# Stage 3 of a two-layer perceiver: keys and queries in a PSUM bank of their own, the end of the attention in two halves, three evictions on ScalarE, the recurrence's first exponentials ahead of the scaling by D

## The chip, the cores and the metric

One core of a Trainium2 chip runs the whole program. The metric is the device time of one execution in microseconds (us). The kernel before took 2087.88 us, the median of three runs that went from 2087.57 to 2094.29.

The core's engines each run their own list of instructions in order: TensorE (PE, with its weight loads shown as PEld), VectorE (DVE), ScalarE (ACT), GpSimd (POOL) and SyncE (SP), which here issues most DMA. Matmul results land in PSUM, which has eight banks of 512 fp32 columns on 128 partitions. "Evicting" a bank means reading it into SBUF.

## The reference

The input x is 64 sequences of 32 tokens with 256 features, 2048 tokens in all; a context of 64 x 257 rows belongs to it. Six residual steps follow one another:

```python
x = x + _L0_xattn_ref(_layernorm(x), ctx, ctx, mask, ...)   # stage 0
x = x + _L0_attn_ref(_layernorm(x), ...)                    # stage 1
x = x + _L0_ffn_ref(_layernorm(x), ...)                     # stage 2
x = x + _L1_xattn_ref(_layernorm(x), ctx, wq, wk, wv, wo, ln_gamma, ln_beta)   # stage 3
x = x + _L1_attn_ref(_layernorm(x), ...)                    # stage 4
x = x + _L1_ffn_ref(_layernorm(x), ...)                     # stage 5
```

The change concerns stages 3 and 4. Stage 3 is grouped-query attention, 16 query heads over 8 key heads of 16 features, with quantised linear maps (each row is scaled to integers up to 127, each weight matrix to -1, 0, 1):

```python
q = bit_linear(x, wq); k = bit_linear(y, wk); v = bit_linear(y, wv)
scores = einsum('bhgnd,bhsd->bhgns', q / 4, k)      # s runs over 257 context rows
out = einsum('bhgns,bhsd->bhgnd', softmax(scores), v)
out = layernorm(out) * ln_gamma + ln_beta
return bit_linear(out, wo)
```

Stage 4 is a selective state-space layer, with 512 channels and 16 states:

```python
h = exp(A * dt) * h + dt * B_t * x_t        # for every time step t
y_t = sum_n h[n] * C_t[n] + D * x_t
y = (y * silu(z)) @ out_proj.T + out_proj_b  # then residual and layernorm
```

## The kernel before

**Tiling.** The 2048 tokens are four blocks of 512 (`NBLK`), a block is four tiles of 128 tokens, and a tile is four sequences ("elements", e) of 32 tokens. `layers` (at the end of the listing) calls the stages block by block. Stages 0 and 1 come first; block 0 of stages 2 and 3 lies beside the last blocks of stage 1. Then stage 3 of block b+1 is called beside the recurrence of block b, and stage 5 of block b-1 after it. Stage 4 has three parts: `ahead` (normalise, project, convolve, step sizes dt), `gates` (silu of z) and `recur`.

**What sets the order.** The kernel is written for a planner that orders each engine's instructions at compile time: what is written earlier has priority, and an instruction whose operands and buffers are free by the planner's costs may come before earlier ones that wait. It puts in all the waits. Every buffer is a tile of a pool under a tag with a number of copies (`bufs`); a tile gets a copy when an earlier tile of the same tag is released.

**PSUM.** From stage 4 on, four pools hold the banks: psh (2, the recurrence's h), psp (1, projections of `ahead` and `gates`), psu (1, stage 5's), psacc (2, stage 5's sums), and, from stage 3 on, ps (2), from which every tile of stage 3 comes.

**Stage 3.** `block` normalises and quantises four tiles into xq and opens o4, the output, in the same buffer (tag xn3, one copy). It then takes nine half-tile steps u. In each, for two elements, `keys` projects keys (kT, L823, evicted on DVE at L825 with the quantisation steps) and values (v, L830, evicted on DVE at L836); `scores` is called for two pairs of heads (matmuls L844, maxima L849 and L851 on DVE, exponentials L855 on ACT); between these two calls, `sums` is called for the step before (transposes L868, copies L870 on ACT, value matmuls L878, evictions od L882 on ACT and L883 on DVE). A new tile begins with `attend`: loads of cq and kb, xqT (L776), q (L781, evicted on DVE at L783), the context's last row (L787 to L795), qT (L800, evicted twice on DVE at L804 into qm) and the last row's scores (L807). `back` ends a tile: softmax denominators, transposes, the write into o4 (L918 to L923). The end of the block, L738 to L764, works on four tiles at once: layernorm, gamma and beta on POOL (L743, L744), quantisation, output projection, residual add (L764).

**Stage 4.** In `recur`, dtx = dt * x is one POOL instruction (L1044), the first step of every sequence is set so that its exponential is zero (L1046), and four ACT instructions scale y by D (L1049). Then for each of 16 states and each pair of channel groups come g on POOL (L1056), exponentials h on ACT (L1060), the scan and the product hc on DVE (L1061, L1062) and the addition to y on POOL (L1063).

Small helpers: `_stats` and `_rsqrt` (L69 to L92) compute means and reciprocal roots with a dozen POOL instructions on four numbers a row; `_norm` (L115) applies them; `_quant_rows` (L340 to L350) scales and rounds.

## Time and profile before

| what | value |
|---|---|
| median of three runs | 2087.88 us |
| the profiled execution's own time | 2087.24 us |
| its span, first to last instruction | 2085.2 us |
| PE busy | 1597.6 us (77%) |
| DVE busy | 1384.2 us (66%) |
| POOL busy | 1049.5 us (50%) |
| ACT busy | 944.1 us (45%) |
| mean granted TensorE clock | 0.832 |

The profile is one execution, recorded by the hardware. A row of a group gives line, engine, operation, output and inputs, shape and count, then the total busy time, the mean duration of one in ns, and the idle time of its engine just before it with what ended that. A row of the timeline gives start and duration in us. A row of one line's instructions gives the shortest, median and longest duration in ns, and the first and last start in us. The busy time of PE includes waiting in its pipeline, so a busy PE need not be at its peak.

### The profile page before, as it was taken

The numbers are of one execution on the slowest core, as the hardware profiler recorded it, in microseconds if no ns is written. First come the engines' busy times: TensorE is split into PE (matmuls) and PEld (weight loads), VectorE is DVE, ScalarE is ACT, GpSimd is POOL, SyncE is SP. The second block draws the span as 40 slices with busy tenths as digits, with TensorE's granted clock in tenths as the row PEclk, the third lists the DMA queues.
The fourth block names the chain that finished last, engine by engine and source line by source line (L and its number), as shares of the span: only waits on it lengthen the run. The fifth ranks groups of instructions, "written<-read, shape, count | busy, mean of one in ns | idle before, by whom it ended". The sixth has DMA issues, their size and how long they took to land. (4 is left out here: it accounts for less than half of the span.)

```text
span 2085.2 us, 20012 instructions
## 1 busy us (share of the span) xinstructions
PE 1597.6 (77%) x6323; PEld 812.4 (39%) x6323; DVE 1384.2 (66%) x2443; ACT 944.1 (45%) x2001; POOL 1049.5 (50%) x1069
## 2 busy tenths in 40 slices
PE   4776967667979788657387789877888787787798
PEld 3333534334545434433144344433344433233343
DVE  4588585765485568888777888775787844877100
ACT  2454352303445264434136466447566536564232
POOL 5344646413121324668724677732677843999100
PEclk9676968778989989657697789988699997899799
DMA  6754333300001010122002232102222212342121
GB/s 221 228 189 141 102 109 104 100 4 21 21 21 42 20 47 21 51 59 63 10 15 83 66 106 86 46 21 87 71 81 71 52 31 77 87 115 72 39 81 41
DMA packets 88376, 151.23 MB, mean 73 GB/s; under 512 B 7740, under 2 KB 52300, under 8 KB 86224
## 3 DMA queue, kind: packets, MB, share of 16 engines
q1 hardware_dynamic: 85428, 148.75, 23.4%
q10 hardware_dynamic: 2844, 1.22, 0.2%
q8 instruction: 50, 0.82, 0.2%
q14 instruction: 54, 0.44, 0.1%
HBM read 139.03 MB, written 10.92 MB: 72 GB/s over the span
## 5 line engine op out<-in xcount | busy, mean ns | idle before, releaser
L1056 POOL TENSOR_TENSOR g<-dtx,bc 128x1024 f32<-128x1024 f32 x128 | 300.4, 2352 | 191.4 <-DVE h L1061 101.7
L1061 DVE TENSOR_TENSOR_SCAN h<-h,g 128x512 f32<-128x512 f32 x256 | 308.1, 1219 | 47.0 <-ACT h L1060 28.7
L1063 POOL TENSOR_TENSOR xc<-xc,hc 128x1024 f32<-128x1024 f32 x128 | 301.0, 2354 | 34.5 <-DVE hc L1062 29.5
L1167 PE MATMUL up<-xT,w 128*128 128x512 f32 x512 | 288.4, 678 | 33.1 <-ACT hid L1169 29.6
L1175 PE MATMUL acc<-hid,w 128*128 128x512 f32 x512 | 258.0, 624 | 19.9 <-ACT hid L1171 19.9
L1060 ACT ACTIVATE h<-dt,A 128x512 f32<-128x512 f32 x256 | 173.9, 692 | 173.5 <-DVE hc L1062 172.3
L1062 DVE TENSOR_TENSOR hc<-h,bc 128x512 f32<-128x512 f32 x256 | 170.1, 681 | 5.8 <-POOL xc L1063 3.0
L1169 ACT ACTIVATE hid<-up,chan 128x512 f32<-128x512 f32 x128 | 87.2, 681 | 179.2 <-PE up L1167 179.2
L855 ACT ACTIVATE p<-sc,nm 128x256 f32<-128x256 f32 x256 | 117.7, 471 | 95.3 <-DVE nm L851 90.5
L1167 PEld LDWEIGHTS up<-xT,w 128*128 128x128 f32 x512 | 97.7, 209 | 157.3 <-issue 84.6
L630 PE MATMUL weps<-we,xT 128*128 128x512 f32 x256 | 140.0, 671 | 23.3 <-DVE x L632 14.7
L868 PE MATMUL pt_ps<-ident,p 128*128 128x128 f32 x512 | 95.9, 325 | 73.6 <-ACT p L855 36.3
L1175 PEld LDWEIGHTS acc<-hid,w 128*128 128x128 f32 x512 | 96.5, 199 | 137.8 <-issue 99.3
L844 PE MATMUL sc<-kT,qm 32*128 32x256 f32 x512 | 133.9, 447 | 4.9 <-DVE kT L825 2.4
L849 DVE TENSOR_REDUCE nm<-sc 128x2 f32<-128x512 f32 x128 | 86.2, 686 | 56.1 <-PE sc L844 55.1
L868 PEld LDWEIGHTS pt_ps<-ident,p 128*128 128x128 f32 x512 | 67.3, 163 | 123.0 <-ACT p L855 79.1
L89 POOL TENSOR_TENSOR rs_t<-rs_r 128x4 f32<-128x4 f32 (+3 forms) x138 | 33.3, 243 | 160.4 <-DVE rs_r L87 142.5
L844 PEld LDWEIGHTS sc<-kT,qm 32*128 32x128 f32 x512 | 82.7, 207 | 62.6 <-issue 10.8
L1188 DVE SCALAR_TENSOR_TENSOR o<-rT,gt,x 128x256 f32<-128x256 f32 x16 | 7.7, 483 | 133.2 <-PE rT L1187 124.0
L870 ACT COPY pt<-pt_ps 128x512 f32<-128x512 f32 x128 | 74.2, 588 | 32.9 <-PE pt_ps L868 32.3
L1044 POOL TENSOR_TENSOR dtx<-xc,dt 128x2048 f32<-128x2048 f32 x4 | 18.0, 4502 | 138.9 <-DVE dt L1030 127.4
L247 POOL TENSOR_TENSOR cT<-cT,scb 128x2056 f32<-128x2056 f32 x16 | 73.2, 4572 | 25.8 <-PE scT_ps L237 11.5
(389 smaller groups left out, 3166.0 us busy)
## 6 DMA issues: line engine op xcount, KB each, us to landing
bc<-rows SPq DMA_DIRECT2D x64, 512.0 KB
w<-in_L_ffn_w_dram SPq DMA_DIRECT2D x64, 512.0 KB
cT<-in_ctxT_dram SPq DMA_DIRECT2D x16, 1028.0 KB
cq<-cq SPq DMA_DIRECT2D x32, 514.0 KB
cn<-in_ctx_dram SPq DMA_DIRECT2D x64, 256.0 KB
scb<-scales SPq DMA_DIRECT2D x16, 514.0 KB
kb<-steps SPq DMA_DIRECT2D x16, 514.0 KB
x<-in_x_dram SPq DMA_DIRECT2D x4, 512.0 KB
```

Source lines behind the costliest of these rows:

```text
L630: nc.tensor.matmul(ps, xT[:, c, r], we[:, c, e : e + 2, :], start=c == 0, stop=c == 1)
L844: nc.tensor.matmul(sc[h][:, f, :], qm[r, e + f].rearrange("p l n g -> p (l n g)"), kTs[e][r, f, :], start=True, stop=True,)
L855: nc.scalar.activation(w_[:, f, h - h0, :], sc[h][:, f, :], AF.Exp, bias=nm[:, e + f, h : h + 1], accum_out=sm[:, e + f, h : h + 1],)
L868: nc.tensor.transpose(pt_ps[:, h, m, :], ws[e0, hp][:, f, h, m * P : (m + 1) * P], k.ident)
L1056: nc.gpsimd.tensor_tensor(g, dtx[:, c2 : c2 + 2], bc[:, 0:1, :].to_broadcast([P, 2, BT]), ALU.mult)
L1060: nc.scalar.activation(h, dt, AF.Exp, scale=A[:, c2 + c, n : n + 1])
L1061: nc.vector.tensor_tensor_scan(h, h, g[:, c, :], 0.0, ALU.mult, ALU.add)
L1062: nc.vector.tensor_tensor(hc[:, c, :], h, bc[:, 1, :], ALU.mult)
L1063: nc.gpsimd.tensor_tensor(y[:, c2 : c2 + 2], y[:, c2 : c2 + 2], hc, ALU.add)
L1167: nc.tensor.matmul(u, w1[e][:, c, q * P : (q + 1) * P], xT[:, c, :], start=c == 0, stop=c == 1)
L1169: nc.scalar.activation(hid[e][:, q, :], u, AF.Identity, bias=b1)
L1175: nc.tensor.matmul(acc[o], w2[e][:, q, o * P : (o + 1) * P], hid[e][:, q, :], start=n == H, stop=n == E * H + H - 1)
```

## The change

- Stage 3 gets a function `pk`, which takes a tile from the pool psp (one bank). The tiles of queries, the last row, keys and values come from it. Where psp is not open yet (block 0), they still come from ps.
- Stage 4's `ahead` takes its tiles from ps instead of psp, and `gates` from psu.
- q, qm and v are evicted on ScalarE: q and qm with one instruction in the place of each one before, v with four instructions of 128 columns in the place of one.
- `sums` handles both elements of a step in one call: one PSUM tile oT for both, two od evictions in the place of four.
- The end of a block becomes a function `finish` over two tiles: it runs to the quantised rows and returns `out`, the output projection and residual add. Tiles 0 and 1 are finished at u = 4 and projected at u = 6; tiles 2 and 3 after the last step.
- dtx is computed in two halves, the first on DVE, the second on POOL. The scaling by D moves into the state loop's first turn, behind the first two channel groups' scans and ahead of their addition to y.
- Small statistics tiles take the number of tiles they are given instead of 4, some get a tag of their own or one copy (rank, rp, rsm, rt), and the quantised end rows yq get a buffer of their own instead of sharing that of xq.

```diff
--- before.py
+++ after.py
...
@@ -700,6 +700,10 @@
+    def pk(shape, name, dt=F32):
+        return k.psp.tile(shape, dt, name=name, tag="p") if k.psp else ps(shape, name, dt)
     def block(b):
...
@@ -728,40 +732,51 @@
                 last.sums(le)
-                last.sums(le + 1)
             if u < 8:
...
                 last.back()
-        ot = [o4[:, j].rearrange("p i l g d -> p (i l g d)") for j in range(4)]
+            if u == 4:
+                ends = [finish(xs, o4, 0)]
+            if u == 6:
+                ends[0]()
+        finish(xs, o4, 2)()
+    def finish(xs, o4, j0):
+        js = range(j0, j0 + 2)
+        ot = [o4[:, j].rearrange("p i l g d -> p (i l g d)") for j in js]
         mv, rstd = _stats(k, ot, "3b")
-        y = o4.rearrange("p j i l g d -> p j (i l g d)")
-        for j in range(4):
-            _norm(k, ot[j], ot[j], mv, rstd, j)
-        nc.gpsimd.tensor_tensor(y, y, gamma.unsqueeze(1).to_broadcast([P, 4, D]), ALU.mult)
-        nc.gpsimd.tensor_tensor(y, y, beta.unsqueeze(1).to_broadcast([P, 4, D]), ALU.add)
-        ss = k.small.tile([P, 4], F32, name="ss", tag="q_ss")
-        yq = k.wk3.tile([P, 4, D], BF16, name="yq", tag="xq", bufs=1)
-        for j in range(4):
-            nc.scalar.activation(yq[:, j, :], y[:, j, :], AF.Square, accum_out=ss[:, j : j + 1])
-        am = k.small.tile([P, 4], F32, name="am", tag="q_am")
+        y = o4[:, j0 : j0 + 2].rearrange("p j i l g d -> p j (i l g d)")
+        for f in range(2):
+            _norm(k, ot[f], ot[f], mv, rstd, f)
+        nc.gpsimd.tensor_tensor(y, y, gamma.unsqueeze(1).to_broadcast([P, 2, D]), ALU.mult)
+        nc.gpsimd.tensor_tensor(y, y, beta.unsqueeze(1).to_broadcast([P, 2, D]), ALU.add)
+        ss = k.small.tile([P, 2], F32, name="ss", tag="q_ss")
+        yq = k.wk3.tile([P, 2, D], BF16, name="yq", tag="yq", bufs=1)
+        for f in range(2):
+            nc.scalar.activation(yq[:, f, :], y[:, f, :], AF.Square, accum_out=ss[:, f : f + 1])
+        am = k.small.tile([P, 2], F32, name="am", tag="q_am2")
         _quant_rows(k, y, 1e-8, yq, am)
-        dy = k.small.tile([P, 4], F32, name="dy", tag="dy")
+        dy = k.small.tile([P, 2], F32, name="dy", tag="dy")
         _rsqrt(k, dy, [(ss, 1.0 / D, RMS_EPS)], "3y")
...
         nc.vector.tensor_scalar(dy, dy, 1e-5, osc, ALU.max, ALU.mult)
-        for j in range(4):
-            yqT_ps = ps([P, 2, P], "yqT_ps", BF16)
-            for c in range(2):
-                nc.tensor.transpose(yqT_ps[:, c, :], yq[:, j, c * P : (c + 1) * P], k.identb)
-            yqT = k.wk3.tile([P, 2, P], BF16, name="yqT", tag="xqT")
-            nc.scalar.copy(yqT, yqT_ps)
-            wo_ps = ps([P, D], "wo_ps")
-            for c in range(2):
-                nc.tensor.matmul(wo_ps, yqT[:, c, :], wo[:, c, :], start=c == 0, stop=c == 1)
-            nc.vector.scalar_tensor_tensor(xs[j], wo_ps, dy[:, j : j + 1], xs[j], ALU.mult, ALU.add)
+        def out():
+            for f in range(2):
+                yqT_ps = ps([P, 2, P], "yqT_ps", BF16)
+                for c in range(2):
+                    nc.tensor.transpose(yqT_ps[:, c, :], yq[:, f, c * P : (c + 1) * P], k.identb)
+                yqT = k.wk3.tile([P, 2, P], BF16, name="yqT", tag="xqT")
+                nc.scalar.copy(yqT, yqT_ps)
+                wo_ps = ps([P, D], "wo_ps")
+                for c in range(2):
+                    nc.tensor.matmul(wo_ps, yqT[:, c, :], wo[:, c, :], start=c == 0, stop=c == 1)
+                x = xs[j0 + f]
+                nc.vector.scalar_tensor_tensor(x, wo_ps, dy[:, f : f + 1], x, ALU.mult, ALU.add)
+        return out
...
@@ -771,18 +786,18 @@
-        xqT_ps = ps([P, 2, P], "xqT_ps", BF16)
+        xqT_ps = pk([P, 2, P], "xqT_ps", BF16)
         for c in range(2):
...
         nc.scalar.copy(xqT, xqT_ps)
-        q_ps = ps([P, D], "q_ps")
+        q_ps = pk([P, D], "q_ps")
         for c in range(2):
...
         q = k.wk3.tile([P, D], F32, name="q", tag="q_ol", bufs=1)
-        nc.vector.tensor_scalar(q, q_ps, dq[:, j : j + 1], None, ALU.mult)
-        last_ps = ps([P, P + 4], "last_ps")
+        nc.scalar.activation(q, q_ps, AF.Copy, scale=dq[:, j : j + 1])
+        last_ps = pk([P, P + 4], "last_ps")
         for c in range(2):
...
@@ -795,14 +810,14 @@
         )
-        qT_ps = ps([P, 2, 4, T], "qT_ps")
+        qT_ps = pk([P, 2, 4, T], "qT_ps")
         for h in range(2):
...
         for l in range(2):
-            nc.vector.tensor_scalar(qm[:, :, l].rearrange("p e n g -> p g e n"), qT_ps, half[:, l : l + 1], None, ALU.mult)
-        sl_ps = ps([P, 4, 4], "sl_ps")
+            nc.scalar.activation(qm[:, :, l].rearrange("p e n g -> p g e n"), qT_ps, AF.Copy, scale=half[:, l : l + 1])
+        sl_ps = pk([P, 4, 4], "sl_ps")
         for e in range(4):
...
@@ -818,12 +833,12 @@
-            kT_ps = ps([P, 2, 2 * P], "kT_ps")
+            kT_ps = pk([P, 2, 2 * P], "kT_ps")
             for c in range(2):
...
             nc.vector.tensor_tensor(kTs[e], kT_ps, kb[:, e : e + 2, 0 : 2 * P], ALU.mult)
-            v_ps = ps([P, 2, 2, P], "v_ps")
+            v_ps = pk([P, 2, 2, P], "v_ps")
             for m in range(2):
...
@@ -833,7 +848,9 @@
             cd = k.cdq[:, :, g].rearrange("p (m e) -> p m e", m=2)[:, :, e : e + 2]
-            nc.vector.tensor_tensor(vs[e], v_ps, cd.unsqueeze(3).to_broadcast([P, 2, 2, P]), ALU.mult)
+            for m in range(2):
+                for f in range(2):
+                    nc.scalar.activation(vs[e][:, m, f, :], v_ps[:, m, f, :], AF.Copy, scale=cd[:, m, f : f + 1])
...
@@ -858,33 +875,34 @@
         def sums(e):
-            e0, f = e - e % 2, e % 2
-            pts = []
-            for hp in range(2):
-                pt_ps = ps([P, 2, 2, P], "pt_ps")
-                for h in range(2):
-                    for m in range(2):
-                        nc.tensor.transpose(pt_ps[:, h, m, :], ws[e0, hp][:, f, h, m * P : (m + 1) * P], k.ident)
-                pt = k.wk3.tile([P, 2, 2, P], F32, name="pt", tag="pt")
-                nc.scalar.copy(pt, pt_ps)
-                pts.append(pt)
-            oT_ps = ps([P, 2, 2 * T], "oT_ps")
-            ob = oT_ps.rearrange("p l q -> p (l q)")
-            for m in range(2):
-                for h in range(4):
-                    r = slice(32 * h, 32 * h + 32)
-                    nc.tensor.matmul(
-                        ob[r], vs[e0][:, m, f, r], pts[h // 2][:, h % 2, m, :],
-                        start=m == 0, stop=m == 1, skip_group_check=True,
-                    )
-            nc.scalar.activation(od4[:, e], oT_ps[:, 0], AF.Copy, scale=half[:, 0:1])
-            nc.vector.scalar_tensor_tensor(od4[:, e], oT_ps[:, 1], half[:, 1:2], od4[:, e], ALU.mult, ALU.add)
+            oT_ps = ps([P, 2, 2, 2 * T], "oT_ps")
+            for f in range(2):
+                pts = []
+                for hp in range(2):
+                    pt_ps = ps([P, 2, 2, P], "pt_ps")
+                    for h in range(2):
+                        for m in range(2):
+                            nc.tensor.transpose(pt_ps[:, h, m, :], ws[e, hp][:, f, h, m * P : (m + 1) * P], k.ident)
+                    pt = k.wk3.tile([P, 2, 2, P], F32, name="pt", tag="pt")
+                    nc.scalar.copy(pt, pt_ps)
+                    pts.append(pt)
+                ob = oT_ps[:, f].rearrange("p l q -> p (l q)")
+                for m in range(2):
+                    for h in range(4):
+                        r = slice(32 * h, 32 * h + 32)
+                        nc.tensor.matmul(
+                            ob[r], vs[e][:, m, f, r], pts[h // 2][:, h % 2, m, :],
+                            start=m == 0, stop=m == 1, skip_group_check=True,
+                        )
+            o2 = od4[:, e : e + 2]
+            nc.scalar.activation(o2, oT_ps[:, :, 0], AF.Copy, scale=half[:, 0:1])
+            nc.vector.scalar_tensor_tensor(o2, oT_ps[:, :, 1], half[:, 1:2], o2, ALU.mult, ALU.add)
...
-            rp = k.small.tile([P, 2, 4, 4], F32, name="rp", tag="rp3")
+            rp = k.small.tile([P, 2, 4, 4], F32, name="rp", tag="rp3", bufs=1)
             rs, pl = rp[:, 0], rp[:, 1]
...
@@ -965,7 +983,10 @@
     def pp(shape, name):
-        return k.psp.tile(shape, F32, name=name, tag="p")
+        return k.ps.tile(shape, F32, name=name, tag="s")
+    def pz(shape, name):
+        return k.psu.tile(shape, F32, name=name, tag="u")
...
@@ -1035,18 +1056,17 @@
         for c in range(C):
-            nc.scalar.activation(v.zs[:, c, :], project(v, C + c, pp), AF.Silu, bias=_chan(k, "L1_attn_in_proj_b", C + c))
+            nc.scalar.activation(v.zs[:, c, :], project(v, C + c, pz), AF.Silu, bias=_chan(k, "L1_attn_in_proj_b", C + c))
...
         dtx = wk.tile([P, C, BT], F32, name="dtx", tag="dtx", bufs=1)
-        nc.gpsimd.tensor_tensor(dtx, y, dt.unsqueeze(1).to_broadcast([P, C, BT]), ALU.mult)
+        for c2, eng in ((0, nc.vector), (2, nc.gpsimd)):
+            yc = y[:, c2 : c2 + 2]
+            eng.tensor_tensor(dtx[:, c2 : c2 + 2], yc, dt.unsqueeze(1).to_broadcast([P, 2, BT]), ALU.mult)
         nc.gpsimd.memset(dt.rearrange("p (b t) -> p b t", t=T)[:, :, 0:1], 1e20)
-        for c in range(C):
-            nc.scalar.activation(y[:, c, :], y[:, c, :], AF.Copy, scale=_chan(k, "L1_attn_D", c))
         bc_rows = v.rows[0 : 2 * N].rearrange("(two n) t -> n two t", two=2)
...
@@ -1060,6 +1080,10 @@
                     nc.vector.tensor_tensor(hc[:, c, :], h, bc[:, 1, :], ALU.mult)
+                if n == 0:
+                    for c in range(c2, c2 + 2):
+                        nc.scalar.activation(y[:, c, :], y[:, c, :], AF.Copy, scale=_chan(k, "L1_attn_D", c))
                 nc.gpsimd.tensor_tensor(y[:, c2 : c2 + 2], y[:, c2 : c2 + 2], hc, ALU.add)
...
@@ -1205,6 +1229,7 @@
     left0, left, right, right2 = ExitStack(), ExitStack(), ExitStack(), ExitStack()
+    k.psp = None
     with left0:
...
```

## The prediction

> **What bounds it now.** I read the page's strip of busy tenths first: no engine is full for long, so the time lies in chains, and these are found by asking where a stage starts and ends. Layer 1's attention (stage 3) handles a block of four token tiles. Its score matmuls (L844), asked for in three stretches of time, give the first and last start of blocks 1, 2 and 3:
>
> ```profile
> L844 PE MATMUL sc<-kT,qm x128: 374/478/792, 747.7 to 976.0; 32*128 32x256 f32 x128
> L844 PE MATMUL sc<-kT,qm x128: 374/374/791, 1076.1 to 1318.2; 32*128 32x256 f32 x128
> L844 PE MATMUL sc<-kT,qm x128: 374/374/791, 1388.7 to 1635.4; 32*128 32x256 f32 x128
> ```
>
> The blocks stand end to end, 313 to 328 us apart, because the next one needs the buffer xn3 that the last one's output o4 holds. Block 1's last residual add (L764) starts at 1043.8, block 2's mean is subtracted (L711) from 1038.5; block 3's from 1368.5. After block 3's last L764 (1690.5) come stage 4 of block 3 (first scan 1750.7, last 1906.8) and stage 5 to the end. So from 704 on the end is set by the attention's own latency, three blocks long, then by a tail of 394 us.
>
> The windows tell how much room an engine has in that chain (columns: window, length, busy us and instructions of PE, weight loads, DVE, ACT, POOL, then granted clock and DMA):
>
> ```profile
> 714.00:1119.00 405.00, 276.30 (x1199) 144.83 (x1198) 318.14 (x605) 169.82 (x379) 214.20 (x214) 0.76 0.16 44
> 1119.00:1691.00 572.00, 464.93 (x1956) 230.70 (x1955) 434.01 (x708) 323.83 (x654) 366.49 (x295) 0.85 0.22 65
> 1691.00:2085.00 394.00, 322.81 (x729) 137.72 (x727) 171.09 (x251) 180.18 (x215) 183.41 (x158) 0.90 0.24 70
> ```
>
> DVE is at 79% in the first, PE at 81% in the second: latency bounds, with one engine not far behind. Within the attention, the timeline of block 3 at the start of its fourth tile shows one line of work through the two banks of the pool ps:
>
> ```profile
> 1575.74 0.28 PE L776 MATMUL xqT_ps<-identb,xq 128*128 128x128 bf16 x2
> ...
> 1582.83 0.59 PE L823 MATMUL kT_ps<-cq,b_L_xattn_wkvT 128*128 128x512 bf16 x2
> ...
> 1585.81 1.67 PE L844 MATMUL sc<-kT,qm 32*128 32x256 f32 x8
> ```
>
> Query preparation takes 7.1 us, keys and values 3.0, and no score runs meanwhile. Each half-tile step (two elements' scores, exponentials, sums) takes some 33 us: 1389 to 1655 over eight.
>
> **The change, part by part (us for one of blocks 1, 2, 3; minus is gain).**
>
> Own bank. Queries, keys and values go to the bank psp. Tile n+1's queries still wait for qm (one buffer), which is free after tile n's last score matmul, so they run under its reductions and exponentials. The three preparations after the first took 6 to 7.1 us in block 3: -20. Keys to scores on the other seven steps, 2 to 3 us: -15. The bounds are 0 (the single bank makes seven evictions serial and nothing is ahead) and -35; I take the full value here and discount below.
>
> Three evictions to ScalarE. DVE loses, per block, 4 q at 0.464, 8 qm at 0.478 and 8 v at 0.683: 11.1 us. ACT gains 4 + 8 of about 0.471 (the 128x256 row of L855) and 32 value pieces. For these the nearest row has half the columns and the same per-partition scale:
>
> ```profile
> L836 DVE TENSOR_TENSOR v<-v_ps,cdq 128x512 f32<-128x512 f32 x32 | 21.9, 683 | 3.9 <-PE v_ps L830 3.9
> L882 ACT ACTIVATE od<-oT_ps,half 128x64 f32<-128x64 f32 x64 | 19.9, 310 | 47.4 <-PE oT_ps L878 43.7 <-PE rt_ps L904 2.7
> L1044 POOL TENSOR_TENSOR dtx<-xc,dt 128x2048 f32<-128x2048 f32 x4 | 18.0, 4502 | 138.9 <-DVE dt L1030 127.4 <-ACT p L855 11.5
> L414 DVE TENSOR_TENSOR d<-hT 128x1024 f32<-128x1024 f32 x8 | 10.2, 1276 | 1.1 <-ACT hT L438 1.1
> ```
>
> The 128x256 row with a scale takes 0.47, the 128x64 row 0.310, so 128 columns are about 0.363: 32 are 11.6 us, against 5.5 on DVE, and one v holds its bank 1.45 us instead of 0.68. The Trainium skill speaks against this (ScalarE: Activation LUTs, Rules for kernel authors: multiplications belong on VectorE), and its figures (What ACT_TABLE_LOAD costs: 280 ns + 0.833 ns an element with one pointer operand, 93 ns of overlap back to back) make an estimate of 4 x 387 - 3 x 93 = 1.27 us, 10.2 for the block. I take the row's 11.6. ACT is busy 324 of 572 us (57%), so 17 more per block, less 2 for merged od, stay under cover; without it they would be the loss, +15.
>
> Sums of two elements in one go. oT now takes one of ps's two banks before the four transposes pt, in the order in which tiles are asked for (in the trace the pool's tiles come strictly in the order of the code). Gains: 16 od evictions on DVE at 0.275 become 8 of some 0.34 (-1.7 busy) and pt's wait for that eviction goes. That wait was 22.4 + 17.2 us over four blocks in the rows of L868, at most -10. Cost: pt has one bank, so a transpose waits for the copy (0.588) before it, twice more a step, 8 x 2 x 0.6 = +10 at most. I take 0. Further, the first pt now needs the second score bank free, two exponentials of 0.47 + 0.20 later: 7 x 1.34 = +9.
>
> End by two tiles. Tiles 0 and 1 are finished in the stream. In block 3 the end ran from the last o (1656.6) to the residual add (1691.0), 34 us. With two tiles: gamma and beta 4.7 to 2.35, norms -0.7, row maximum -0.6, quantising -0.8, two of four output projections (1.2 to 3.4 us each) -2.5: -7. The extra half repeats 24 POOL operations of 0.2 (+5 busy) and some 3 us of small DVE operations, both inside the stream; on the path they would be +8, and they are the reason to take no more than -7.
>
> Stage 4's tiles change place. The tiles of `ahead` now come from ps, in order before the next block's scores. Before, block 3's scores ran from 1389 while `ahead` projected until its last ssm matmul at 1414; now the first score waits for that tile's eviction. Bounds 0 and +26 (1389 to 1415); step 1 of the block was at 1408 anyway, so I take +10. Two banks instead of one for four projections save `ahead` about -4, counted in the tail only. `gates` goes to psu behind stage 5's last transposes (until 1745 for block 3): +5, tail only.
>
> Recurrence by halves. dtx was 4.5 us on POOL. Without contention the halves take max(1.28 by L414, 2.35 by L1056) = 2.35, saving 2.15. The trace shows what DVE does beside it: a DVE instruction with a 128x4 tile and two SBUF inputs lasts until POOL is done.
>
> ```profile
> 1430.93 4.50 POOL L1044 TENSOR_TENSOR dtx<-xc,dt 128x2048 f32<-128x2048 f32 x1 [45.41 <-DVE dt L1030]
> ...
> 1431.69 3.75 DVE L851 TENSOR_TENSOR nm<-nm,nsl 128x4 f32<-128x4 f32 x1
> ```
>
> The Trainium skill says the same as a rule against the split (SBUF — State Buffer, Who interferes with whom: a VectorE instruction with two SBUF inputs contends with GpSimd reading SBUF). By it the halves are serial, 1.28 + 2.35 = 3.6, saving 0.9. I take 0.9. D's four scalings (2.56 at 1745.5) leave the place ahead of the first exponential: -2.6 more, so -3.5 a block. In blocks 1 and 2 the attention covers it, so it counts once, in the tail; without the cover it would gain three times.
>
> **The sum.** One block: -20 - 15 + 9 + 0 - 7 + 10 = -23; three, -69. Not all arrives: the attention shares in-order DVE, ACT and PE with recurrence and stage 5. PE's highest share in a long stretch was 90% (106.53 of 119 us, from 451 to 570); at 88% the 465 us of the second window need 528, a limit of -44 for two blocks against -46 asked. So I count 60%: -41. Tail: -3.5 - 4 + 5 = -2.5, taken as -3. Block 0 keeps all tiles in ps and gets the longer value eviction (8 x 0.77 = +6) and first pt (+9), less its end (-7); the last stage 1, ending at 714 on its own, covers most: +2. Total -42. The profiled execution took 2087.24 (span 2085.2, 2.04 around it): 2045. The median shown, 2087.88, is 0.6 above it.
>
> **Rivals.** *The ps line gets longer* (22%). oT holds one bank for the whole pair, and each of four pt copies queues on ACT behind gelu (1.91), table loads (1.28) and the new evictions. It decides once a step's sums grow by 4 us beyond what I count (they take 8 to 14 now), since 8 x 4 exceeds the 23 + 9 of a block. At +5, with scores behind `ahead` at +19, a block gives -23 + 40 + 9 = +26; at 60% of three, +47, less 3, up to 2131; half of it, 2108. For it: rows show copies waiting on ACT and the pool order is strict; against it: pt's wait for od goes. *Recurrence sets the pace* (18%): DVE's scans with POOL's products take 157 us alone (block 3) but 205 to 214 beside attention; then only DVE's relief counts, some 8 us a block, at 60% with the tail: 2070. *All of it arrives* (12%): -69, and `ahead` hidden beside the recurrence, another -20: 1998. *Nothing* (6%): gains and waits cancel, 2087. The planner's freedom to reorder speaks for it.
>
> **The numbers.** My case, 2045 (2020 to 2062), has 42%. A measurement tells 0.3% (6.3 us) from no change. Faster: 42 + 18 + 12 = 72%; same 6%; slower 22%. The range 1988 to 2108 leaves out some 4% below and half of the slower case, 11%, above, the rest being shares of each at its edge.
>
> **What would show it.** Right: the score starts of blocks 1 to 3 some 300 us apart instead of 313 to 328; keys' matmuls before the last exponentials of the step ahead; step length under recurrence below 30 us; the first scan within 8 us of dt. Wrong: pt's transposes waiting for pt copies for more than 20 us in all, first scores waiting for ssm's eviction, a v eviction well over 1.5 us, or DVE idle no shorter while blocks keep their length.

## The result, and the profile after

The changed kernel took 2106.61 us, the median of seven runs (2097.02 to 2113.77), against 2087.88 for the kernel before, the median of seven runs of the same series. The ratio is 1.0095, with a 95% interval of 1.0073 to 1.0118: slower by some 19 us, where 2045 had been predicted. The profiled execution is the fastest of the seven (2097.02 us, span 2095.2), so sums made from the trace explain 10 us, and the other 9 lie between executions.

The scores of blocks 1, 2 and 3, as in the prediction (first and last start in us):

```profile
L861 PE MATMUL sc<-kT,qm x128: 374/478/791, 762.6 to 959.4; 32*128 32x256 f32 x128
L861 PE MATMUL sc<-kT,qm x128: 374/374/791, 1052.9 to 1301.9; 32*128 32x256 f32 x128
L861 PE MATMUL sc<-kT,qm x128: 374/478/791, 1377.0 to 1609.0; 32*128 32x256 f32 x128
```

The attention did get earlier: block 3's last score starts at 1609.0 instead of 1635.4. Between the first scores of blocks 1 and 2 lie 290 us, as the prediction's sign asked (some 300), but between those of blocks 2 and 3 lie 324, where it had been 313. That the attention got earlier shows in the last residual adds of block 3 too, first the kernel before and then the changed one:

```profile
L764 DVE SCALAR_TENSOR_TENSOR x<-wo_ps,dy,x x4: 472/482/486, 1685.9 to 1690.5; 128x256 f32<-128x256 f32 x4
```

```profile
L777 DVE SCALAR_TENSOR_TENSOR x<-wo_ps,dy,x x4: 459/472/483, 1587.4 to 1662.7; 128x256 f32<-128x256 f32 x4
```

The first add of the changed kernel, at 1587.4, is the half that is now finished in the stream. The last add is 28 us earlier than before, and yet the span is 10 us longer. Cutting the span at the last residual add of each block shows where that happens:

| us | up to block 0's end | block 1 | block 2 | block 3 | from there to the end | span |
|---|---|---|---|---|---|---|
| before | 712.2 | 331.6 | 333.9 | 312.8 | 394.7 | 2085.2 |
| after | 717.5 | 296.9 | 330.6 | 317.7 | 432.5 | 2095.2 |
| difference | +5.3 | -34.7 | -3.3 | +4.9 | **+37.8** | +10.0 |

Block 1 gained more than predicted, and stage 5 begins only at 1086 us, behind it. Blocks 2 and 3, which have stage 5 beside them, gained nothing. The tail, which the prediction held to be 394 us less 3, grew by 38. The windows of the changed kernel (columns as in the prediction):

```profile
714.00:1119.00 405.00, 298.80 (x1304) 158.00 (x1302) 332.38 (x615) 200.56 (x470) 238.83 (x268) 0.74 0.17 49
1119.00:1691.00 572.00, 448.98 (x1833) 224.77 (x1832) 418.93 (x673) 321.45 (x669) 360.85 (x351) 0.84 0.21 59
1691.00:2095.00 404.00, 326.84 (x737) 141.64 (x736) 165.32 (x219) 180.16 (x211) 176.99 (x132) 0.90 0.24 71
```

In the first window PE did 23 us more than before. In the second it did 16 less and DVE 15 less: no engine is fuller there, they stand idle for longer. What was not done there is stage 5's work. Its hidden tiles (32 a block, 128 in all) that had been evicted when block 3's attention ended, in the kernel before (up to 1690.5) and in the changed one (up to 1662.7):

```profile
L1169 ACT ACTIVATE hid<-up,chan x58: 662/687/718, 1155.8 to 1688.7; 128x512 f32<-128x512 f32 x58
```

```profile
L1193 ACT ACTIVATE hid<-up,chan x51: 667/687/709, 1115.4 to 1651.0; 128x512 f32<-128x512 f32 x51
```

Seven hidden tiles fewer are done, and they have to be done in the tail. The tail can be cut once more, at the last scan of block 3's recurrence (first and last scan of that recurrence, then the hidden tiles evicted up to the last scan; the kernel before, then the changed one):

```profile
L1061 DVE TENSOR_TENSOR_SCAN h<-h,g x64: 1199/1220/1232, 1750.7 to 1906.8; 128x512 f32<-128x512 f32 x64
L1169 ACT ACTIVATE hid<-up,chan x94: 662/680/718, 1155.8 to 1906.1; 128x512 f32<-128x512 f32 x94
```

```profile
L1081 DVE TENSOR_TENSOR_SCAN h<-h,g x64: 1195/1222/1232, 1720.6 to 1883.7; 128x512 f32<-128x512 f32 x64
L1193 ACT ACTIVATE hid<-up,chan x83: 666/677/709, 1115.4 to 1883.0; 128x512 f32<-128x512 f32 x83
```

From the attention's end to the first scan it takes 58 us (60 before), from the first scan to the last 163 (156), and from the last scan to the end 211 (178). So 33 of the 38 us lie behind the last scan, where 45 hidden tiles are left instead of 34. The recurrence itself is early: its last scan starts 23 us sooner.

A further thing is seen between the stages 5 of two blocks. The timeline of the changed kernel around the end of block 1's stage 5:

```profile
1762.58 0.48 DVE L1212 SCALAR_TENSOR_TENSOR o<-rT,gt,x 128x256 f32<-128x256 f32 x1 [0.18 <-PE rT L1211]
1763.11 3.78 PE L997 MATMUL inps<-xT,w_L_attn_in_projT 128*128 128x512 f32 x4 [0.58 <-DVE o L1212]
1763.14 1.28 ACT L1059 ACT_TABLE_LOAD   x1
...
1766.93 0.69 ACT L1059 ACTIVATE zs<-inps,chan 128x512 f32<-128x512 f32 x1 [2.51 <-PE inps L997]
1767.64 1.28 ACT L1080 ACT_TABLE_LOAD   x1
...
1780.67 0.66 PE L1145 MATMUL t_ps<-ident,xn 128*128 128x128 f32 x4 [2.02 <-ACT zs L1059]
```

The four tiles of `gates` now stand in stage 5's bank: they wait for the last rT of block 1 although block 3's attention has been done since 1663, and block 2's first t_ps waits for them. The pause between two stages 5, from the end of the last rT to the first t_ps, is 31.1 and 18.1 us; before it was 9.0 and 6.9. Block 2's stage 5 thus begins at 1780.7, 60 us behind the first scan of block 3; before it was at 1752.4, 2 us behind it. That is the stretch in which most of the 11 tiles are lost: at the first scan only four fewer were done (60 instead of 64).

### The profile page after: what moved, and what is told of

Its sections match the earlier page's. It is cut to its first block, busy times and chain, and to the rows that moved or that the text cites. A ratio compares the mean times of both kernels' runs of the same rounds, so it can differ in the third digit from the quotient of the medians.

```text
span 2095.2 us, 20140 instructions
## 1 busy us (share of the span) xinstructions
PE 1608.8 (77%) x6323; PEld 822.2 (39%) x6323; DVE 1366.9 (65%) x2383; ACT 980.5 (47%) x2137; POOL 1063.0 (51%) x1173
## 5 line engine op out<-in xcount | busy, mean ns | idle before, releaser
L1199 PE MATMUL acc<-hid,w 128*128 128x512 f32 x512 | 262.9, 634 | 27.1 <-ACT hid L1195 27.1
L861 PE MATMUL sc<-kT,qm 32*128 32x256 f32 x512 | 143.1, 476 | 32.6 <-DVE od L901 13.1
L630 PE MATMUL weps<-we,xT 128*128 128x512 f32 x256 | 145.9, 690 | 18.8 <-DVE x L632 9.1
L89 POOL TENSOR_TENSOR rs_t<-rs_r 128x4 f32<-128x4 f32 (+4 forms) x162 | 37.8, 235 | 199.4 <-DVE rs_r L87 166.6
L887 PE MATMUL pt_ps<-ident,p 128*128 128x128 f32 x512 | 94.4, 323 | 32.6 <-ACT p L872 14.2
L530 POOL TENSOR_TENSOR kk<-kk 128x512 f32<-128x512 f32 x32 | 34.1, 1072 | 108.4 <-ACT kk L529 108.4
```

The lines of the kernel that those rows point to most:

```text
L630: nc.tensor.matmul(ps, xT[:, c, r], we[:, c, e : e + 2, :], start=c == 0, stop=c == 1)
L861: nc.tensor.matmul(sc[h][:, f, :], qm[r, e + f].rearrange("p l n g -> p (l n g)"), kTs[e][r, f, :], start=True, stop=True,)
L887: nc.tensor.transpose(pt_ps[:, h, m, :], ws[e, hp][:, f, h, m * P : (m + 1) * P], k.ident)
L1199: nc.tensor.matmul(acc[o], w2[e][:, q, o * P : (o + 1) * P], hid[e][:, q, :], start=n == H, stop=n == E * H + H - 1)
```

## The experiments

Each ratio is to the kernel before, measured in the same series; 0.1% is 2.1 us. "Tail" is, as above, the span from block 3's last residual add to the end, of the profiled execution.

### First round: gates, sums, evictions

I had three suspects: P, `gates` in stage 5's bank; S, the sums of two elements in one go; E, the evictions on ScalarE. Three kernels undo one of them each in the changed kernel, and one puts the first into the kernel before.

```diff
# a1_gates_psh: changed kernel, gates from psh
     def pz(shape, name):
-        return k.psu.tile(shape, F32, name=name, tag="u")
+        return k.psh.tile(shape, F32, name=name, tag="h")
```

> The changed kernel with one line different: the four projections of gates take their tile from psh (two banks, idle between two recurrences) instead of psu, stage 5's only bank. Theory P (stage 5's chain through psu sets the end, and gates stand in it): stage 5's first transposes of block 2 no longer wait for gates of block 3 (in the changed kernel they lie at 1763 to 1780 us, between stage 5 of block 1 and of block 2), nor those of block 1 for gates of block 2 (1432 to 1457); the kernel gains 20 to 40 us on the changed one, 2065 to 2085. Theory S (the sums with one bank for the transposes, or the evictions on ScalarE, eat the gain): within 8 us of the changed kernel, 2098 to 2115.

Measured: 2080.94 us, 0.9970 [0.9957, 0.9984]. The pauses fell to 4.0 and 4.5 us, and the stretch behind the last scan from 211 to 188.

```diff
# a2_old_sums: changed kernel, sums(e) of before, twice a step
                 last.sums(le)
+                last.sums(le + 1)
```

> The changed kernel with sums as before: one oT and two evictions for each element, so that the transposes have both banks of ps. Theory S: 15 to 30 us faster than the changed kernel, 2075 to 2092. Theory P: within 8 us of it, 2098 to 2115, for stage 5 still waits in psu.

Measured: 2086.93 us, 1.0012 [0.9997, 1.0027].

```diff
# a3_dve_evict: changed kernel, q, qm and v evicted on VectorE (v's lines shown)
-            for m in range(2):
-                for f in range(2):
-                    nc.scalar.activation(vs[e][:, m, f, :], v_ps[:, m, f, :], AF.Copy, scale=cd[:, m, f : f + 1])
+            nc.vector.tensor_tensor(vs[e], v_ps, cd.unsqueeze(3).to_broadcast([P, 2, 2, P]), ALU.mult)
```

> The changed kernel with q, qm and v evicted on VectorE as before. Theory E (ScalarE's new evictions delay exponentials and copies): 10 to 25 us faster than the changed kernel, 2080 to 2096. Theory P: within 8 us of it or up to 10 us slower, as VectorE gets 11 us a block back: 2098 to 2117.

Measured: 2101.74 us, 1.0077 [1.0048, 1.0106]; against the changed kernel's 1.0095 no difference can be told.

```diff
# b1_gates_psu: kernel before, gates from psu
-project(v, C + c, pp), AF.Silu
+project(v, C + c, pz), AF.Silu       # pz: psu, tag "u"
```

> The kernel before with one part of the change alone: gates take their tiles from psu. Theory P: slower than before by 15 to 35 us, 2103 to 2123, with stage 5's first transposes of blocks 1 and 2 behind gates. Theory S and E: within 6 us of before, 2082 to 2094.

Measured: 2089.10 us, 1.0016 [1.0001, 1.0031]. The pauses are there (34.2 and 27.3 us), but hardly the time: 60 hidden tiles were done at block 3's end instead of 58, and the stretch behind the last scan is 183 us, not 211. So the pauses alone do not make a kernel slower. In the changed kernel, however, P and S could each be undone for 26 and 17 us, each to about the time of before, which says that neither was the one cause.

### Is the attention's gain there at all?

The next two kernels leave stage 5 of blocks 0, 1 and 2 out, in both versions:

```diff
-            s5(b - 1)
+            at = (b - 1) * BT
+            k.nc.sync.dma_start(out[at : at + BT, :].rearrange("(j p) d -> p j d", p=P), k.x[b - 1])
```

> The kernel before with stage 5 of blocks 0, 1 and 2 left out (their rows of the output are stage 4's x, written by a DMA), so that only block 3's stage 5 remains: what is computed is less, on purpose. Theory 'stage 5's own chain sets the end' (C): with it gone, the end follows from the attention. Stage 5 of the other blocks also took PE, DVE and ACT from the attention, so 1950 to 2050 us; the number that counts is its difference to the same cut of the changed kernel. Rival 'the attention's line in ps sets the end' (A): the same range; it differs in the next run.

> The changed kernel with the same cut (stage 5 of blocks 0 to 2 left out, less is computed). Theory C: the gain that the attention did make comes to light, so it is 15 to 40 us faster than the same cut of the kernel before (the last scan ended 23 us earlier in the profile of the full kernels). Rival A, the line in ps got longer: equal to the cut of before or slower by up to 20 us.

Measured: 2027.90 us (0.9717 [0.9688, 0.9745]) and 1983.60 us (0.9502 [0.9478, 0.9526]). **Without stage 5 beside it the change gains 44 us**, slightly over the 42 predicted for the whole kernel. The last residual adds of block 3 (c1, then c2), and the span cut as above:

```profile
L764 DVE SCALAR_TENSOR_TENSOR x<-wo_ps,dy,x x4: 474/484/484, 1639.8 to 1643.2; 128x256 f32<-128x256 f32 x4
L777 DVE SCALAR_TENSOR_TENSOR x<-wo_ps,dy,x x4: 469/476/484, 1548.4 to 1615.0; 128x256 f32<-128x256 f32 x4
```

| us | up to block 0's end | block 1 | block 2 | block 3 | tail | span |
|---|---|---|---|---|---|---|
| c1, before without stage 5 | 709.8 | 331.7 | 303.0 | 298.7 | 380.9 | 2024.1 |
| c2, after without stage 5 | 730.2 | 304.0 | 294.0 | 286.8 | 369.8 | 1984.8 |
| difference | +20.4 | -27.7 | -9.0 | -11.9 | -11.1 | -39.3 |

Blocks 2 and 3 gain 9 and 12 us when nothing else wants the engines, and the tail gets shorter. With stage 5 they gain nothing and the tail gets 38 longer. So the gain is lost only beside stage 5: shown by its removal, not by argument. Through which engine or buffer it is lost, the removal doesn't show. It also took away load (PE was busy for 309 and 312 us of the window from 1119 to 1691, instead of 465 and 449), and the granted clock in that window was 0.61 and 0.59, instead of 0.85 and 0.84.

Two more kernels of this round tried whether P and S add up, and controlled for psh:

> The changed kernel with two parts undone: gates' four tiles from psh, and the sums of two elements in one go undone (one element at a time, as before). Alone they gave -26 and -20 against the changed kernel. If they act at different places (gates between two stages 5, sums in the attention's steps) they add up: 2058 to 2070. If both remove the same delay (the end is set by one chain at a time) the two together give no more than the larger: 2075 to 2085.

> The kernel before with one edit: gates' four tiles from psh instead of psp. A control for the earlier run that did this to the changed kernel. If that gain came from taking gates out of stage 5's bank, nothing is to be gained here: 2080 to 2094. If psh is simply a better place for gates than any other, it is faster here too, by 10 us or more.

c3 measured 2108.32 us, 1.0105 [1.0077, 1.0134]: undoing both parts, which gave 26 and 17 us one at a time, gave nothing. c4, the kernel before with `gates` from psh, measured 2069.82 us, 0.9918 [0.9888, 0.9947]. So a gain from psh is also there without the change (17 us), and a1's 26 can't be put down to the changed kernel's psu alone. But psh is not better everywhere: with the sums of before in the changed kernel it cost 19 us (a2 to c3).

### The parts one by one

With `gates` in psh as the common base (c4, 0.9918), each part of the change alone. Only the copies of small tiles (one instead of more for rank, rp, rsm and rt) had no run of their own; d2 and e3 have them too, and so do the kernels made from the changed one (a1 to a3, c2, c3, e1, e2, e4, f2).

```diff
# d1_bank: queries, keys and values from psp, ahead's tiles from ps
-            kT_ps = ps([P, 2, 2 * P], "kT_ps")
+            kT_ps = pk([P, 2, 2 * P], "kT_ps")     # and so the other six
     def pp(shape, name):
-        return k.psp.tile(shape, F32, name=name, tag="p")
+        return k.ps.tile(shape, F32, name=name, tag="s")
# d2_finish: the end by two tiles
+            if u == 4:
+                ends = [finish(xs, o4, 0)]
+            if u == 6:
+                ends[0]()
+        finish(xs, o4, 2)()
# d3_recur: dtx by halves on two engines, D behind state 0
-        nc.gpsimd.tensor_tensor(dtx, y, dt.unsqueeze(1).to_broadcast([P, C, BT]), ALU.mult)
+        for c2, eng in ((0, nc.vector), (2, nc.gpsimd)):
# d4_evict: q, qm and v on ScalarE;  f1_sums: sums of two elements in one go
```

> The kernel before with gates from psh (2069.8, ratio 0.992) plus one part of the change: queries, keys and values from psp, ahead's tiles from ps. The prediction gave this part -20 - 15 + 10 a block. Theory H, 'one part does harm beside stage 5': this is it, since ahead's tiles now stand in the scores' order: 10 to 25 us slower than 2069.8. Theory L, 'no part is harmful, the gain is lost because stage 5 sets the end': within 8 us of 2069.8. Theory of the prediction: 2030 to 2050.

> The kernel before with gates from psh (2069.8) plus the end of the attention by two tiles. Theory H: it isn't this part, 2062 to 2078, some gain of x earlier by 5 to 10 us a block that stage 5 doesn't let through. Theory L: 2062 to 2078. If the end by two tiles (5 us more POOL work a block, and small operations of DVE inside the stream) is the harm: 2080 to 2095.

> The kernel before with gates from psh (2069.8) plus the recurrence begun by halves and ahead of D. The prediction gave it -3.5, in the tail only. Theories H and L: 2062 to 2072. If it does harm (its DVE half takes DVE from the attention beside it): 2075 to 2085.

> The kernel before with gates from psh (2069.8) plus the three evictions on ScalarE. The prediction gave it 0 under cover, +15 a block without. Theories H and L: 2065 to 2077. If ScalarE sets the pace beside stage 5 (its gelu and hidden evictions): 2080 to 2100.

> The kernel before with gates from psh (2069.8, ratio 0.992) plus the sums of two elements in one go, the last of the parts not run alone. The prediction gave it 0, with -10 and +10 as bounds, and +9 a block for the first transposes. Theory S, 'the sums in one go cost': the gains of the other three parts (0.9896, 0.988, 0.9904 alone) would put the changed kernel without the end by two tiles at 0.9846, and it measured 0.992 with them, so the sums cost some 0.7%: 2075 to 2095. Rival T, 'no part costs more, the gains of the parts are one and the same slack': 2060 to 2074.

| kernel | us | ratio to before | against c4 |
|---|---|---|---|
| d1_bank | 2063.66 | 0.9896 [0.9876, 0.9915] | -0.2% |
| d2_finish | 2098.19 | 1.0067 [1.0044, 1.0090] | **+1.5%** |
| d3_recur | 2059.46 | 0.9880 [0.9852, 0.9909] | -0.4% |
| d4_evict | 2066.61 | 0.9904 [0.9882, 0.9926] | -0.1% |
| f1_sums | 2081.52 | 0.9963 [0.9949, 0.9978] | +0.45% |

Only d2 stands out by far: it is 31 us slower than c4, where a difference of two such kernels is known to about 8 us. f1 costs 9, give or take 7; the other three can't be told from nothing. In d2 the attention ends 26 us later and the tail is 7 longer. The part of a block before the last score is what grows. Block 3's scores of c4 and of d2:

```profile
L844 PE MATMUL sc<-kT,qm x128: 374/374/791, 1380.1 to 1627.1; 32*128 32x256 f32 x128
```

```profile
L856 PE MATMUL sc<-kT,qm x128: 373/375/792, 1389.3 to 1670.1; 32*128 32x256 f32 x128
```

281 us instead of 247; from the last score to the last residual add it then took 38 us instead of 54. The end itself got 17 us shorter, more than the 7 that I counted, and the stream 34 us longer. In blocks 1 and 2 the ends got 5 and 15 us shorter and the streams 8 and 18 longer. What the end's operations wait for, by the groups of c4 and of d2 (idle time of the engine before them, and what ended it):

```profile
L748 ACT ACTIVATE yq<-o 128x256 bf16<-128x256 f32 x16 | 6.4, 403 | 23.6 <-POOL o L744 14.4 <-DVE rs_r L87 9.2
L115 DVE TENSOR_SCALAR o<-o,mv,rstd 128x256 f32<-128x256 f32 x16 | 5.5, 410 | 6.9 <-POOL rstd L92 6.9
```

```profile
L115 DVE TENSOR_SCALAR o<-o,mv,rstd 128x256 f32<-128x256 f32 x16 | 11.0, 726 | 16.4 <-POOL rstd L92 16.4
L755 ACT ACTIVATE yq<-o 128x256 bf16<-128x256 f32 x16 | 6.5, 408 | 39.3 <-POOL o L751 34.7 <-DVE rs_r L87 4.7
```

ScalarE stands 39 us before yq instead of 24, and VectorE 16 before the norms instead of 7, and a norm lasts 726 ns in the mean instead of 410. These instructions wait for POOL's chain, now twice a block and in the middle of the attention's steps: 16 + 10 us of waiting and 5 of busy time. That comes to 31 us, but it does not show that this is the loss. Waits on two engines can lie side by side; ScalarE's wait before the copies yqT fell at the same time, from 48 us to 24 (the rows of c4 and of d2):

```profile
L760 ACT COPY yqT<-yqT_ps 128x256 bf16<-128x256 bf16 x16 | 6.0, 372 | 48.2 <-PE yqT_ps L758 47.0 <-DMA bx<-in_L_attn_x_proj_b_dram 1.1
L769 ACT COPY yqT<-yqT_ps 128x256 bf16<-128x256 bf16 x16 | 5.9, 370 | 24.1 <-PE yqT_ps L767 24.0
```

Nor are the longer norms the loss: only four of d2's sixteen were stretched, and in e3 below none was (at most 415 ns), though that kernel is slower still.

### Undoing the end by two tiles, and moving it

> The changed kernel with one part undone: the end of the attention again by four tiles, at the end of the block. Theory F, 'the end by two tiles is what makes the change slower' (with gates from psh it alone cost 31 us): 2106.6 - 31, so 2068 to 2085, faster than before. Rival P, 'gates in stage 5's bank sets it' : the pauses between the stages 5 stay, so 2095 to 2108.

e1, the changed kernel with the end by four tiles again, measured 2084.59 us, 0.9978 [0.9965, 0.9991]. Undoing this one part gives 24 us back and makes the rest of the change as fast as before or slightly faster. Rival P falls as what makes the changed kernel slower than before: the pauses are still 27.7 and 17.1 us. They are not free, though: the stretch behind the last scan is still 211 us, and what e1 gained lies ahead of it. The wait before yq is nearly as long as in d2, too, so it is no mark of the loss:

```profile
L751 ACT ACTIVATE yq<-o 128x256 bf16<-128x256 f32 x16 | 6.4, 404 | 35.5 <-POOL o L747 30.7 <-DVE rs_r L87 4.8
```

> The same with gates' tiles from psh too, so all parts but the end by two tiles and gates' place. Theory F with gains that add up from 2069.8 (bank -5, recurrence -8, evictions -3, and sums): 2035 to 2058, the fastest of all. If the gains of the parts are one and the same slack: 2058 to 2070. Rival P: no faster than the changed kernel with gates from psh, 2081.

e2 measured 2074.71 us, 0.9920 [0.9896, 0.9944]: no faster than c4. So in the full kernel all the other parts together gain nothing. Against a1, which has the end by two tiles besides, e2 is 10 us faster.

```diff
# e3_end2_late: d2 with both halves asked for behind the last sums
-            if u == 4:
-                ends = [finish(xs, o4, 0)]
-            if u == 6:
-                ends[0]()
+        finish(xs, o4, 0)()
         finish(xs, o4, 2)()
```

> The kernel before with gates from psh and the end by two tiles (2098.2), but both halves asked for behind the last sums, as the end stood before: the same added work, not in the stream. Theory F1, 'operations of the end stand in the attention's stream, and the engines that take instructions in order wait for their chain': back to 2064 to 2080. Theory F2, 'the added work itself (24 more operations of POOL a block, two chains for one)': 2085 to 2100.

e3 measured 2118.87 us, 1.0124 [1.0098, 1.0150], worse than both theories allowed. The trace shows that it didn't do what it was meant to:

```profile
L752 ACT ACTIVATE yq<-o x16: 398/416/417, 626.5 to 1716.9; 128x256 bf16<-128x256 f32 x16
```

The first yq of block 0 still starts at 626.5, 60 us before that block's last score: the planner takes the first half's chain as soon as its tiles are there. The first half's output projections, whose tiles stand in the order of ps, moved behind: in block 3 its first residual add starts at 1707.9, behind the last score (1684.4). Place and added work remain unseparated.

> The changed kernel without stage 5 of blocks 0 to 2 (their rows of the output are stage 4's x, so less is computed) and with the end by four tiles again. With the end by two tiles this cut took 1983.6. If the end by two tiles does harm only beside stage 5: 1990 to 2010, since without stage 5 the shorter end is a gain. If it does harm there too: 1950 to 1980.

e4 measured 1978.28 us, 0.9466 [0.9440, 0.9491], against c2's 0.9502: without stage 5 the end by two tiles costs 0.4% and not 1.2 to 1.5%, and that difference is no larger than its own interval (0.35%). Most of its harm needs a crowded core.

The end by two tiles did harm in every pair of full kernels that differ in it: 31 us (c4 and d2, with the small tiles' copies), 24 (e1 and after), 10 (e2 and a1), and 37 (f2 below and c3). That it costs time beside stage 5 is shown; by which wait, it is not.

> The kernel before with gates from psh and the three parts that alone were faster: own bank, recurrence by halves, evictions on ScalarE; the end by four tiles and the sums one element at a time stay. Theory S: the gains add up, 0.982 to 0.987, so 2045 to 2058, the fastest of all. Rival T: not below the best part alone, 2058 to 2072.

f2, the base c4 with the three harmless parts (and the small tiles in one copy), measured 2075.68 us, 0.9928 [0.9904, 0.9953]. Its attention is the fastest of all full kernels: block 3's last residual add starts at 1635.1 us, 55 earlier than before. It is no faster than c4. The hidden tiles done by then, in f2 and in d3:

```profile
L1181 ACT ACTIVATE hid<-up,chan x52: 664/687/719, 1134.7 to 1634.9; 128x512 f32<-128x512 f32 x52
```

```profile
L1175 ACT ACTIVATE hid<-up,chan x62: 662/687/722, 1139.9 to 1671.8; 128x512 f32<-128x512 f32 x62
```

d3 ends its attention 37 us later, with ten more hidden tiles done, and is the faster kernel. Its median is also the lowest of the full kernels that I ran: the kernel before with `gates` from psh and the recurrence begun by halves, 2059.46 us, 1.2% faster than before. d1 and d4 can't be told from it.

In f2 most of the gain is lost ahead of block 3's recurrence: its first scan starts 96 us after the attention's end, in c4 65 and in the changed kernel 58. In a1 and e2, which also have the other parts and `gates` in psh, it is 86 and 82. What that scan waits for was not followed up.

### What all full kernels have in common

Eleven of the 17 kernels that leave nothing out, in the order of their tails:

| kernel | block 3's attention ends | hidden tiles done then | tail | hidden tiles done at the last scan | last scan to end | span |
|---|---|---|---|---|---|---|
| d4_evict | 1693 | 64 | 375.5 | 96 | 174.9 | 2068.5 |
| d3_recur | 1672 | 62 | 381.7 | 95 | 172.6 | 2053.7 |
| c4_before_gates_psh | 1681 | 62 | 382.4 | 96 | 176.3 | 2063.8 |
| e3_end2_late | 1730 | 61 | 389.4 | 95 | 174.8 | 2119.7 |
| d2_finish | 1708 | 60 | 389.6 | 94 | 180.0 | 2097.2 |
| before | 1691 | 58 | 394.7 | 94 | 178.4 | 2085.2 |
| c3_psh_old_sums | 1689 | 55 | 412.7 | 91 | 185.7 | 2102.1 |
| e1_after_end4 | 1656 | 51 | 424.9 | 83 | 211.3 | 2081.0 |
| a1_gates_psh | 1651 | 55 | 429.9 | 91 | 187.6 | 2080.9 |
| after | 1663 | 51 | 432.5 | 83 | 211.5 | 2095.2 |
| f2_bank_recur_evict | 1635 | 52 | 439.3 | 91 | 187.2 | 2074.4 |

A straight line through the 17 full kernels' profiles has 4.7 us of tail for each hidden tile that is not done when the attention ends (correlation 0.95; the largest distance from the line is 14 us). For after against before that makes 7 x 4.7 = 33 of the 38 us. Part of this holds by construction, as an attention that ends later leaves more tiles done and a shorter tail. The last scan is the better place to cut: behind it there are 3.0 us for each tile not done (correlation 0.99, largest distance 4 us), so 11 tiles make the 33 us. And a short tail is not a fast kernel: e3 and d2 have one and are slow, because their attention ends late.

## Why the prediction was wrong

**The step that failed** is the first one: "from 704 on the end is set by the attention's own latency, three blocks long, then by a tail of 394 us". The three blocks were to gain 41 us and gained 33 in sum, which is partly luck: block 1, with no stage 5 beside it, gained 35 where 14 were counted, and blocks 2 and 3 nothing where 28 were counted. The tail was taken as a constant with -3 for small things, and it measured +38. It is not a constant: 33 of the 38 us lie behind the last scan and go with the 11 hidden tiles that stage 5 had not done by then. Stage 5 comes after the attention in priority and lives on what the attention leaves. An attention that is ready 28 us sooner, and a last scan that is 23 sooner, leave it less time, and here it also did less with the time that it had: the first hidden tile of the whole program came 40 us earlier than before, and yet fewer were done. The second step that failed is the end by two tiles, -7 a block, without which the changed kernel was 24 us faster (e1). The prediction's own windows held the warning: with PE at 81% and DVE at 76% in the stretch where all three stages run, I asked how far the attention could go before PE is full, and not whose work would be put off.

**Own bank, -35 less 10 a block.** On c4 it gave -0.2%, not to be told from nothing. In the trace the attention did get faster with it: it ended 21 us earlier, all of it in block 1 (301.6 us instead of 327.3), while block 3 took 11 us more and the tail grew from 382 to 398.

**Evictions on ScalarE, 0 under cover.** Not contradicted: -0.1% alone, give or take 0.4%, and undoing them in the changed kernel changed nothing that can be told. The row of v:

```profile
L853 ACT ACTIVATE v<-v_ps,cdq 128x128 f32<-128x128 f32 x128 | 36.5, 370 | 27.4 <-PE v_ps L845 27.3
```

0.370 us against 0.363 estimated. But four in a row hold the bank 1.14 us, not 1.45, since they overlap by some 0.11 each:

```profile
1552.67 1.14 ACT L853 ACTIVATE v<-v_ps,cdq 128x128 f32<-128x128 f32 x4 [3.02 <-PE v_ps L845]
```

The estimate of 1.27 made from the Trainium skill (ScalarE: Activation LUTs, What ACT_TABLE_LOAD costs) was nearer than my row. To put multiplications on ScalarE against its rule (ScalarE: Activation LUTs, Rules for kernel authors) cost nothing that can be told here.

**Sums in one go, 0, and +9 a block for the first transposes.** That is 27 us over three blocks, 16 at 60%; alone on c4 it measured +9, give or take 7, which doesn't contradict it. The transposes' wait for a copy, which I had named as a sign of error above 20 us, came to 13.8 us on PE and 28.1 on its weight loads:

```profile
L887 PE MATMUL pt_ps<-ident,p 128*128 128x128 f32 x512 | 94.4, 323 | 32.6 <-ACT p L872 14.2 <-ACT pt L889 13.8 <-DVE h L1081 4.3
L887 PEld LDWEIGHTS pt_ps<-ident,p 128*128 128x128 f32 x512 | 67.7, 163 | 79.0 <-ACT p L872 30.1 <-ACT pt L889 28.1 <-issue 19.0
```

Yet all that PE waited before these transposes fell, from 73.6 us to 32.6, as the waits for other things became shorter. And the part's effect depends on what stands around it: taking it out gained 17 us with `gates` in psu (a2), lost 28 with `gates` in psh (a1 to c3), and with the end by four tiles besides it changed nothing that can be told (e2 to f2).

**End by two tiles, -7 a block.** Wrong in sign: 31 us in all on c4, 24 in the changed kernel. I counted the repeated small operations by their busy time and let them vanish in the stream, with +8 a block as the worst case. 31 us over four blocks is +8 a block in the mean, but that agreement is chance: block 3's stream alone grew by 34 us, and its end became 17 shorter. What holds the stream up is not known; the waits for POOL's chain are one candidate, and the rows speak for and against it.

**`gates` behind stage 5's transposes, +5 in the tail.** The price alone is about right (+3 us in b1, give or take 3), by luck: the pauses are 34 and 27 us, and nearly all of that time is made up elsewhere. In the changed kernel it was much dearer: the stretch behind the last scan was 204 to 211 us in the four kernels that have `gates` in psu with the rest of the change (after, a2, a3, e1), and 173 to 188 in all the other full ones. What I missed was another place: psh gives 17 us in a kernel that changes nothing else.

**Recurrence by halves, -3.5 once.** Not contradicted: -0.4% +- 0.4%. VectorE's half and POOL's half ran one behind the other, as expected:

```profile
1391.78 1.23 DVE L1067 TENSOR_TENSOR dtx<-xc,dt 128x1024 f32<-128x1024 f32 x1
1391.89 3.32 POOL L1067 TENSOR_TENSOR dtx<-xc,dt 128x1024 f32<-128x1024 f32 x1 [38.53 <-DVE dt L1051]
```

They end 3.43 us after the first start, against 3.6 by the shared-port rule of the Trainium skill (SBUF — State Buffer, Who interferes with whom) and 2.35 had they been free of each other. The first scan starts at 1397.70, 6 us behind dt.

**The rivals.** Half of "the ps line gets longer" came to 2108, and 2106.6 came, but by chance and not by its mechanism: the blocks did not get longer, they got 33 us shorter in sum. "Recurrence sets the pace" and "all of it arrives" did not come. That the place of the end could move to stage 5 was not among the rivals, though stage 5's end of block 2 stood at 1943 us, only 35 behind the last scan.

**What stays open:** why the parts do not add up. The lines above say where the time is, not why c3 or f2 came out as they did. Each edit can make the planner choose another order on five engines. The same move of `gates` from psu or psp to psh gave -17 us (c4), -26 (a1), -12 (e1 to e2) and +19 (a2 to c3), so a difference of 10 to 20 us between two neighbouring kernels may be such a change of order and nothing else. This rival was not tested. The small tiles' single copies were not run alone either.

## What to carry to other kernels

When a stage of high priority is made faster, ask what the stages of lower priority have done by the time that it ends: leave them out in both versions, and the difference tells whether a gain is absent or given back. Do not treat the tail as a constant; here, behind the last scan, it was 3.0 us for each tile that had been put off. And when a chain is moved into the middle of other work, measure both sides of it: here the end of a block got 17 us shorter and the work ahead of it 34 us longer.

## What was not expected of the hardware

A VectorE instruction that takes one tile and two numbers per row can be held up through several of POOL's instructions in a row. Two of stage 5's norms (L115), in the changed kernel, one behind the other (shortest, median and longest duration in ns):

```profile
L115 DVE TENSOR_SCALAR xn<-x,mv,rstd x2: 401/3135/5869, 1766.4 to 1772.2; 128x256 f32<-128x256 f32 x2
```

```profile
1765.15 4.67 POOL L1076 TENSOR_TENSOR g<-dtx,bc 128x1024 f32<-128x1024 f32 x2
1769.76 2.36 POOL L1087 TENSOR_TENSOR xc<-xc,hc 128x1024 f32<-128x1024 f32 x1
```

The first norm lasted 5.87 us and ended 0.15 us behind the third of POOL's products; the second took 0.40. Three of d2's sixteen norms of the attention's end were stretched in this way, beside one product each (1.1 to 2.4 us, again ending 0.15 us behind it); one of the kernel before was too. The granted TensorE clock also went with the work: 0.82 to 0.84 in the full kernels' profiles, 0.72 to 0.73 without most of stage 5.
